# Normalised pixels in a ring of six parts, more buffers, a third accumulated tap in some jobs, and 6 of 11 bands of one convolution chunk on TensorE

## The chip, the core and the metric

The kernel runs on one core of a Trainium2 chip. The core has five engines that follow their own instruction queues in order: TensorE (PE in the profile; its weight loads are PEld), VectorE (DVE), ScalarE (ACT), GpSimd (POOL) and SyncE (SP). Waits on semaphores tie the queues together. The metric is the device time of one execution in microseconds (us).

## What is computed

The input is x, 16 images of 128 channels and 96 x 96 pixels in float32. Per image:

```python
xn1 = layernorm(x, ln1_w, ln1_b)                    # over the 128 channels of each pixel
q, k, v = xn1 @ wq.T, xn1 @ wk.T, xn1 @ wv.T        # 8 heads of 16 channels
attn = softmax(einsum('bhcn,bhdn->bhcd', l2norm(q), l2norm(k)) * 16**-0.5)   # over pixels n
x = x + (attn @ v) @ wp.T
xn2 = layernorm(x, ln2_w, ln2_b)
h1 = einsum('bchw,oc->bohw', xn2, w_in)             # 128 -> 512 hidden channels
h2 = depthwise_conv3x3(h1, w_dw)                    # 9 taps per channel, zero padding
x = x + einsum('bchw,oc->bohw', gelu(h2), w_out)    # 512 -> 128
```

The attention is between channels, so all of it is held in a Gram matrix of 128 x 128 per image, and its result is one 128 x 128 matrix per image that is multiplied with the normalised pixels.

## The kernel before

An image is cut into 8 bands of 12 rows, and a band into 3 units of 4 rows (384 pixels). The 512 hidden channels are 4 chunks of 128. One band and one chunk make a job. The program is laid down by a planner: each operation is registered with a place on a common scale, an estimated duration, the tokens that it reads and writes, and the buffers that it takes; a list scheduler then fixes the order of each engine's queue. The places are the table AT, in units of jobs. They are fixed in the source; nothing is scheduled while the kernel runs.

For each pixel block the first and second normalisation (suffix _a and _b) run: transpose (`forth`), statistics on VectorE, a power on GpSimd, scaling on ScalarE, transpose back (`back`), and a copy into the padded image (`place`). The first one also feeds the Gram matrix (`gram`). After the attention of an image, `mix` multiplies its first-normalised pixels with the attention's matrix and adds x. The second normalisation writes its pixels over the first ones.

```python
PE_CHUNK = 3
PE_BANDS = (0, 2, 4, 6)
PE_OF = 7
# ...
DMA_TAPS = (1, 2)
QT = 4
H_BANKS = 4
X1_BUFS, XB_BUFS, PR_BUFS, H3_BUFS, ZT_BUFS = 2, 5, 4, 9, 3
# ...
    xns = [pad.tile([P, HP * WP + 2], F32, tag=f"xn{k}", name=f"xn{k}") for k in range(min(B, 2))]
# ...
    def interior(i, u):
        return window(xns[i % 2], 1 + u * UR, UR, 1)
```

The padded images `xns` are thus two buffers of a whole image each, used in turn. The convolution of a job has nine taps. Tap 0 and the taps in DMA_TAPS are products of ScalarE; the products of DMA_TAPS are summed by accumulating transfers (SBUF to SBUF, issued by GpSimd), and the other six taps are multiply-and-add instructions of VectorE:

```python
        def product(t):
            if t == 0:
                to = h3_of(g, n)
            else:
                to = d["pr", t] = prp.tile([P, BR, W], F32, tag="pr", name=f"pr_{g}_{n}_{t}")
            nc.scalar.activation(to, shifted(t), AF.Copy, scale=dw[:, n, t : t + 1])

        def tap(t):
            h3 = h3_of(g, n)
            nc.vector.scalar_tensor_tensor(h3, shifted(t), dw[:, n, t : t + 1], h3, ALU.mult, ALU.add)

        def add_products(t):
            to = d["pr", DMA_TAPS[0]] if t != DMA_TAPS[0] else h3_of(g, n)
            nc.gpsimd.dma_start(out=to, in_=d["pr", t], accum_op=ALU.add)
# ...
        last = j == len(jobs) - 1
        dma_taps = () if last else DMA_TAPS
        left = [t for t in range(1, 9) if t not in dma_taps]
# ...
        act(t_act(BR * W, 1), at("product", j), lambda: product(0), h1, h3)
        for k, t in enumerate(dma_taps):
            jk = j + STEP["products"] * k
            act(t_act(BR * W, 1), at("products", jk), lambda t=t: product(t), h1, [("pr", (jn, t))])
        pr = [("pr", (jn, t)) for t in dma_taps]
        for k, t in enumerate(dma_taps[1:]):
            add(at("add_last", j), lambda t=t: add_products(t), [pr[1 + k]], [pr[0]])
        for k, t in enumerate(left):
            dve(t_dve(BR * W), at("tap", j + STEP["tap"] * k), lambda t=t: tap(t), h1, h3, True)
        if dma_taps:
            add(at("add_first", j), lambda: add_products(DMA_TAPS[0]), [pr[0]], h3)
```

The chunk 3 of some bands goes another way: the 1 x 1 product and the 3 x 3 convolution are one matmul per tap, nine accumulating in PSUM, with no work for VectorE.

```python
        for t in range(9):
            dy = t // 3
            zs = z_units(i, r0 + dy, r0 + dy + UR)
            pe(t_mm(UT), at("conv", p + STEP["conv_tap"] * t), lambda t=t: product(t), [*zs, ("w", "conv")], [pc])
        act(t_act(UT), at("conv_gelu", p), gelu, [pc], [("h3", (g, PE_CHUNK), s)])
# ...
    def by_pe(g):
        return g % PE_OF in PE_BANDS

    NG = B * NB
    jobs, first = [], []
    for g in range(NG):
        first.append(len(jobs))
        jobs += [(g, n) for n in range(NCH) if n != PE_CHUNK or not by_pe(g)]
```

Then `ffn_out` multiplies the four chunks of a unit with w_out, VectorE adds the result to x, and a band is stored.

Of the kernel before, what the change touches and what calls it, by code (L numbers as in the profile page):

```python
# [20 lines left out]
PE_BANDS = (0, 2, 4, 6)  # L21
PE_OF = 7
TINY = 1e-20
DMA_TAPS = (1, 2)
QT = 4
H_BANKS = 4
X1_BUFS, XB_BUFS, PR_BUFS, H3_BUFS, ZT_BUFS = 2, 5, 4, 9, 3
IN_TURN = ("tr", "h3", "pr", "xb", "x1")
AT = dict(
    weights=0.9, zeros=6.55, load_a=-14.05, forth_a=-8.8, stats_a=-11.5, variance_a=-13.4, power_a=3.35,  # L30
    shift_a=-4.85, scaled_a=-0.8, gram=-2.9, back_a=-19.8, place_a=-18.9, attention=-9.75, mix=-10.05,
    residual=-13.2, mixed=-4.5, add_x=4.65, forth_b=-6.15, stats_b=1.25, variance_b=-4, power_b=-19,
    shift_b=-16.6, scaled_b=0.85, back_b=-14.75, place_b=-1.75, halo=1.55, hidden=-0, kept=-5.25,
    product=-4.6, products=2.35, add_last=-9.55, tap=6, add_first=25.15, gelu=-2.6, conv=1.9,
    conv_gelu=-2.9, out=2.85, add=5.05, store=1.6,
)
STEP = dict(hidden=0.1, products=0.5, tap=0.166, conv=1.6, conv_tap=0.03, out=0.8, out_part=0.05)
# [3 lines left out]
WAIT = dict(POOL=350, SP=1300, ACT=1300)  # L41
T_ADD, T_MOVE = 3100, 1800


class Plan:
# [44 lines left out]
    def order(self):  # L90
# [38 lines left out]
        def dispatch(engine, time):  # L129
            queue = queues[engine]  # L130
            while queue:
                item = heapq.heappop(queue)
                k = item[1]
                lacks = room(k)
                if lacks is None:
                    break
                waiting.setdefault(lacks, []).append(k)
            else:
                return
            o = ops[k]  # L140
            starts[k] = time
            idle[engine] = False
            for t in o[5]:
                self.slot[t] = free[t[0]].pop(0)
                if t[0] in IN_TURN:
                    turn[t[0]].pop()
                    wake(t[0], time)
            ns, result, own = o[1], o[6], o[7]
            if o[8]:
                self.dma = max(time + ns + WAIT[engine], self.dma) + o[8]  # L150
                result = own = self.dma + result - time
            elif engine == "POOL":
                rest = self.two - time
                ns, result = (ns, result) if rest <= 0 else (rest + 705, rest + result)
                own = result
            if o[9]:
                self.two = time + ns + 35
            push(time + own, "own", k)
            push(time + ns, "idle", k)
            push(time + result, "done", k)  # L160
# [39 lines left out]
def tile_restormer_block(  # L200
# [33 lines left out]
    HP, WP = H + 2, W + 1  # L234
    D = C // HEADS
    assert PE_CHUNK == NCH - 1 and BR * W >= 8 * P and QT % 2 == 0 and NU * TPU % QT == 0 and C == P and UT % P == 0 and H % BR == 0 and NCH == 4
# [22 lines left out]
    mhalf = const.tile([P, QT], F32, name="mhalf")  # L259
# [25 lines left out]
    xns = [pad.tile([P, HP * WP + 2], F32, tag=f"xn{k}", name=f"xn{k}") for k in range(min(B, 2))]  # L285
# [20 lines left out]

    def interior(i, u):
        return window(xns[i % 2], 1 + u * UR, UR, 1)
# [21 lines left out]
    def z_units(i, r0, r1):  # L330

        lo, hi = min(max(r0 - 1, 0), H - 1) // UR, min(r1 - 2, H - 1) // UR
        return [("z", i % 2, u) for u in range(lo, hi + 1)]
# [29 lines left out]
    def zeros(p):  # L363


        def around(t, r):
            if r == HP:
                nc.gpsimd.memset(t[:, :WP], 0.0)
                nc.gpsimd.memset(t[:, (r - 1) * WP : r * WP], 0.0)
            nc.gpsimd.memset(t[:, : r * WP].rearrange("p (r w) -> p r w", w=WP)[:, :, :1], 0.0)  # L370
            nc.gpsimd.memset(t[:, r * WP :], 0.0)

        for t in zT_bufs:
            op("POOL", 300, at("zeros", p - 1), lambda t=t: nc.gpsimd.memset(t[:, :, P:], 1.0), [], [("w", "ones")], 500)
        for t, r in [(xns[0], HP)] + [(t, BR + 2) for t in h1s] + [(xn, HP) for xn in xns[1:]]:
            op("POOL", 1000, at("zeros", p), lambda t=t, r=r: around(t, r), [], [("w", "in")], 1200)

# [97 lines left out]
    def norm(i, second, place_of):  # L475
# [8 lines left out]
        def x2(s, u):  # L484
# [21 lines left out]
            ins = [("z", i % 2, u), ("m", i)]  # L506
# [10 lines left out]
        def pixels(s, q):  # L517

            d = {}
            tiles = range(q * QT, (q + 1) * QT)  # L520
            early = i == 0 and (not second or q < EARLY)
# [3 lines left out]
            def forth():  # L525
                if early:
                    d["pT"] = bank((name, q)).rearrange("p (t c) -> p t c", c=P)
                else:
                    d["pT"] = p_tr.tile([P, QT, P], F32, tag="tr", name=f"pT_{name}_{q}")
                for t in tiles:  # L530
                    b, j = divmod(t, TPB)
                    xt = (xbs if x_key(i, b, second) == "xb" else x1s)[i, b]
                    nc.tensor.transpose(d["pT"][:, t - tiles[0], :], xt[:, j * P : (j + 1) * P], ident)  # L533

            def stats(j):

                if j == 0:
                    d["st"] = small.tile([P, QT // 2, 6], F32, tag="st", name=f"st_{name}_{q}")
                nc.vector.bn_stats(  # L539
                    d["st"][:, j, :], d["pT"][:, 2 * j : 2 * j + 2, :].rearrange("p t c -> p c t")  # L540
                )

            def variance():
                d["mv"] = d["st"].rearrange("p j (t v) -> p (j t) v", v=3)
                ve = d["ve"] = small.tile([P, QT], F32, tag="ve", name=f"ve_{name}_{q}")
                nc.vector.tensor_scalar(ve, d["mv"][:, :, 2], 1.0 / C, EPS, ALU.mult, ALU.add)  # L546

            def power():
                rstd = d["rstd"] = small.tile([P, QT], F32, tag="rstd", name=f"rstd_{name}_{q}")
                nc.gpsimd.tensor_tensor(rstd, d["ve"], mhalf, ALU.pow)  # L550

            def shift():
                nb = d["nb"] = small.tile([P, QT], F32, tag="nb", name=f"nb_{name}_{q}")
                nc.vector.scalar_tensor_tensor(nb, d["mv"][:, :, 1], -1.0, d["rstd"], ALU.mult, ALU.mult)  # L554
                if by_dve:
                    take_zT()

            def take_zT():
                zTs[q] = zT_bufs[plan.slot["zT", (name, q)]]

            def also_scaled():
                for j in range(by_dve):
                    nc.vector.tensor_scalar(  # L563
                        zTs[q][:, j, :P], d["pT"][:, j, :], d["mv"][:, j, 1:2], d["rstd"][:, j : j + 1],
# [3 lines left out]
            def scaled():  # L568
                if not by_dve:
                    take_zT()  # L570
                zT = zTs[q]
                for j in range(by_dve, QT):
                    nc.scalar.activation(  # L573
                        zT[:, j, :P], d["pT"][:, j, :], AF.Identity,
                        bias=d["nb"][:, j : j + 1], scale=d["rstd"][:, j : j + 1],
                    )

            def gram():
                if q == 0:
                    grams[i] = p_g.tile([P, 4 * P], F32, tag="g", name=f"g_{i}")  # L580
                for t in tiles:
                    zt = zTs[q][:, t - tiles[0], :]
                    nc.tensor.matmul(  # L583
                        grams[i][:, : P + 1], lhsT=zt[:, :P], rhs=zt, start=(t == 0), stop=(t == NU * TPU - 1)
                    )

            tr, bt, zt = (key_, (name, q)), ("batch", (name, q)), ("zT", (name, q))
            units = {t // TPU: None for t in tiles}
            pe(110 * QT, at("forth" + ab, s), forth, [xtok(u) for u in units], [tr])
            for j in range(QT // 2):  # L590
                dve(341, at("stats" + ab, s), lambda j=j: stats(j), [tr], [bt])
            dve(80, at("variance" + ab, s), variance, [], [bt])
            op("POOL", 848, at("power" + ab, s), power, [], [bt], 881 + SLACK)
            dve(80, at("shift" + ab, s), shift, [], [bt, (*zt, 2)] if by_dve else [bt])
            if by_dve:
                dve(by_dve * 240, at("scaled" + ab, s), also_scaled, [tr, bt], [(*zt, 0)])
            act((QT - by_dve) * 343, at("scaled" + ab, s), scaled, [tr, bt], [(*zt, 1)])
            if not second:
                pe(QT * 220, at("gram", s), gram, [(*zt, 0), (*zt, 1), ("w", "ones")], [("g", i)])

        def channels(s, u):
# [14 lines left out]

            pb = ("bk", (name, u))
            quads = {(u * TPU + j) // QT: None for j in range(TPU)}
            pe(110 * TPU, at("back" + ab, s), back, [("zT", (name, q), k) for q in quads for k in range(2)], [pb])
            act(t_act(UT, 1) - 43 if second else t_copy(UT), at("place" + ab, s), place, [pb, ("w", "shift")], [("z", i % 2, u)])  # L620
# [7 lines left out]
        for q in range(NU * TPU // QT):  # L628
            pixels(place_of(q * QT), q)
            while u < NU and (u + 1) * TPU <= (q + 1) * QT:  # L630
# [3 lines left out]
    def attention(s, i):  # L634
# [4 lines left out]
        v = {}  # L639

# [4 lines left out]
        def ps(shape, tag):  # L645

            c = columns[tag]
            v[tag] = grams[i][: shape[0], c : c + shape[1]]
            return v[tag]

        def step(engine, ns, also=()):
            def add(f):
                op(engine, ns, s, f, [("w", "qk")], [("g", i), ("m", i), *also], ns + 200 + SLACK)
# [4 lines left out]
        @step("DVE", 210)  # L658
# [49 lines left out]
        @step("POOL", 848)  # L708
# [57 lines left out]
    def conv_job(j, g, n):  # L766

        i, b = divmod(g, NB)
        xn, r0 = xns[i % 2], b * BR
# [44 lines left out]
        dma_taps = () if last else DMA_TAPS  # L814
# [3 lines left out]
        for k, (r, e) in enumerate(chunks):  # L818
            ph = ("h", (jn, r))
            jk, zs = j + STEP["hidden"] * k, z_units(i, r0 + r, r0 + e)  # L820
# [20 lines left out]
    def by_matmuls(p, g, s):  # L841

        i, b = divmod(g, NB)
        xn = xns[i % 2]
        d = {}
        r0 = b * BR + s * UR
# [14 lines left out]
        for t in range(9):  # L861
            dy = t // 3
            zs = z_units(i, r0 + dy, r0 + dy + UR)
# [34 lines left out]
    def by_pe(g):  # L898
        return g % PE_OF in PE_BANDS
# [15 lines left out]
    for i in range(B):  # L915
# [4 lines left out]
        attention(at("attention", start2), i)  # L920
        norm(i, True, lambda t: start2 + band * t / TPB)
# [37 lines left out]
```

## Time and profile before

| | |
|---|---|
| device time, median of 3 executions | 4420.35 us (4417.46 to 4422.78) |
| span of the profiled execution | 4419.5 us |
| PE busy | 4309.8 us, 17782 matmuls |
| DVE busy | 4271.7 us, 5681 instructions |
| ACT busy | 4059.8 us, 7071 instructions |
| POOL busy | 1884.1 us, 1620 instructions |
| data moved by DMA | 744.52 MB, 168 GB/s on average |

A row of groups in the profile gives the source line, the engine, the operation, what it writes and reads, how often (x), its busy time in us and the mean duration of one in ns, and then the idle time of its engine just before it and who ended that. A row of waits gives who waited for whom: us in total, how often, the longest. A row of the timeline gives the start, the length, engine, line and operation, with equal neighbours merged (x6 is six instructions); in square brackets is the idle time before it. One instruction may begin before the one before it is shown as ended, so lengths of neighbours overlap. Line 803 is a tap on VectorE, 799 a product on ScalarE, 807 the accumulating transfers, 811 the GELU, 783 the hidden product and 788 its copy into the padded band, 853 the convolution on TensorE with its GELU in 859, 876 the product with w_out, and 883 the last add.

### The profile page before, as it was taken

The numbers are of one execution on the slowest core, as the hardware profiler recorded it, in microseconds if no ns is written. First come the engines' busy times: TensorE is split into PE (matmuls) and PEld (weight loads), VectorE is DVE, ScalarE is ACT, GpSimd is POOL, SyncE is SP. The second block draws the span as 40 slices with busy tenths as digits, with TensorE's granted clock in tenths as the row PEclk, the third lists the DMA queues.
The fourth block names the chain that finished last, engine by engine and source line by source line (L and its number), as shares of the span: only waits on it lengthen the run. The fifth ranks groups of instructions, "written<-read, shape, count | busy, mean of one in ns | idle before, by whom it ended". The sixth has DMA issues, their size and how long they took to land. (4 is left out here: it accounts for less than half of the span.)

```text
span 4419.5 us, 53360 instructions
## 1 busy us (share of the span) xinstructions
PE 4309.8 (98%) x17782; PEld 2750.3 (62%) x17782; DVE 4271.7 (97%) x5681; ACT 4059.8 (92%) x7071; POOL 1884.1 (43%) x1620
## 2 busy tenths in 40 slices
PE   7999999999999999999999999999999999999997
PEld 6656666666666666666666666666666666666554
DVE  6999999999999999999999999999999999999998
ACT  4999999999999999999999999999999999989885
POOL 3444444344444444444444444444435444444331
PEclk9999999999999999999999999999999999999998
DMA  2778888787888878788887887878888788878886
GB/s 78 160 162 177 172 175 179 166 181 158 182 172 172 183 166 176 168 171 180 167 176 167 179 173 163 181 167 179 173 171 177 167 181 168 171 171 162 171 166 134
DMA packets 183635, 744.52 MB, mean 168 GB/s; under 512 B 21312, under 2 KB 22720, under 8 KB 183360
## 3 DMA queue, kind: packets, MB, share of 16 engines
q0 software_dynamic: 143856, 589.30, 70.7%
q1 hardware_dynamic: 37152, 151.01, 9.4%
q8 instruction: 140, 2.29, 0.2%
q10 hardware_dynamic: 2352, 0.81, 0.1%
q14 instruction: 135, 1.11, 0.1%
HBM read 148.85 MB, written 75.50 MB: 51 GB/s over the span
## 5 line engine op out<-in xcount | busy, mean ns | idle before, releaser
L803 DVE SCALAR_TENSOR_TENSOR h<-h,dw,h 128x1152 f32<-128x1152 f32 x2636 | 3651.3, 1405 | 5.4 <-ACT h L799 1.0
L853 PE MATMUL h<-xn,comp 128*128 128x384 f32 x3942 | 1422.7, 486 | 8.2 <-ACT x L500 5.0
L799 ACT ACTIVATE pr<-h,dw 128x1152 f32<-128x1152 f32 x876 | 1131.1, 1301 | 31.3 <-DMA pr<-pr 30.7
L876 PE MATMUL h<-h,woutT 128*128 128x384 f32 x3072 | 1116.1, 492 | 41.3 <-ACT h L788 17.7
L783 PE MATMUL h<-xn,winT 128*128 128x384 f32 (+1 forms) x2634 | 1034.2, 500 | 5.7 <-ACT h L859 2.4
L853 PEld LDWEIGHTS h<-xn,comp 128*128 128x128 f32 x3942 | 719.4, 189 | 465.7 <-issue 17.1
L876 PEld LDWEIGHTS h<-h,woutT 128*128 128x128 f32 x3072 | 562.6, 192 | 400.9 <-ACT h L788 27.9
L807 POOL DMA_DIRECT2D h<-pr x438 | 408.1, 932 | 845.8 <-issue 154.3
L788 ACT COPY h<-h 128x384 f32<-128x384 f32 (+1 forms) x1317 | 655.0, 532 | 90.8 <-PE h L783 68.8
L807 POOL DMA_DIRECT2D pr<-pr x438 | 404.3, 923 | 752.0 <-ACT pr L799 611.8
L550 POOL TENSOR_TENSOR rstd_b<-ve_b,mhalf 128x4 f32<-128x4 f32 x288 | 524.1, 1820 | 380.4 <-DVE ve_b L546 354.1
L550 POOL TENSOR_TENSOR rstd_a<-ve_a,mhalf 128x4 f32<-128x4 f32 x288 | 509.2, 1773 | 388.4 <-DVE ve_a L546 376.1
L783 PEld LDWEIGHTS h<-xn,winT 128*128 128x128 f32 x2634 | 474.7, 190 | 304.6 <-issue 35.9
L811 ACT ACTIVATE h<-h 128x1152 f32<-128x1152 f32 x441 | 529.4, 1201 | 71.4 <-DMA h<-pr 68.6
L799 ACT ACTIVATE h<-h,dw 128x1152 f32<-128x1152 f32 x439 | 569.8, 1298 | 4.9 <-PE h L876 1.1
L573 ACT ACTIVATE zT<-pT_b,nb_b,rstd_b 128x128 f32<-128x128 f32 x1132 | 438.8, 510 | 14.6 <-DVE nb_b L554 13.6
L573 ACT ACTIVATE zT<-pT_a,nb_a,rstd_a 128x128 f32<-128x128 f32 x1080 | 417.5, 508 | 22.3 <-DVE nb_a L554 19.4
L583 PEld LDWEIGHTS g<-zT 128*128 128x128 f32 x2304 | 291.2, 191 | 40.2 <-issue 2.1
L583 PE MATMUL g<-zT 128*128 128x129 f32 x2304 | 304.8, 274 | 0.2 <-DVE zT L563 0.2
L491 PE MATMUL h<-xn,mwT 128*128 128x384 f32 x768 | 286.2, 489 | 3.2 <-ACT h L788 1.7
L613 ACT ACTIVATE xn<-pB_b,b 128x384 f32<-128x384 f32 x384 | 242.7, 632 | 24.4 <-PE pB_b L609 23.4
L539 DVE BATCH_NORM_STATS2 st_b<-pT_b 128x6 f32<-128x256 f32 x566 | 236.2, 420 | 6.2 <-PE pT_b L533 5.7
(111 smaller groups left out, 3237.3 us busy)
## 6 DMA issues: line engine op xcount, KB each, us to landing
pr<-pr POOLq DMA_DIRECT2D x438, 576.0 KB, 5.4
h<-pr POOLq DMA_DIRECT2D x438, 576.0 KB, 6.2
x<-in_x_dram SPq DMA_DIRECT2D x128, 576.0 KB, 5.5
out_dram<-x SPq DMA_DIRECT2D x127, 576.0 KB, 3.7
x<-in_x_dram POOLq DMA_DIRECT2D x123, 576.0 KB, 7.2
out_dram<-x SPq DMA_DIRECT2D x3, 192.0 KB, 1.8
weights<-in_L_conv_w_in_dram ACTq DMA_DIRECT2D x1, 256.0 KB, 10.6
weights<-in_L_conv_w_out_dram ACTq DMA_DIRECT2D x1, 256.0 KB, 10.7
```

Of the source, the lines that this page charges most:

```text
L491: nc.tensor.matmul(rows(pm), lhsT=mats[i][0], rhs=interior(i, u), start=True, stop=True)
L550: nc.gpsimd.tensor_tensor(rstd, d["ve"], mhalf, ALU.pow)
L573: nc.scalar.activation(zT[:, j, :P], d["pT"][:, j, :], AF.Identity, bias=d["nb"][:, j : j + 1], scale=d["rstd"][:, j : j + 1],)
L583: nc.tensor.matmul(grams[i][:, : P + 1], lhsT=zt[:, :P], rhs=zt, start=(t == 0), stop=(t == NU * TPU - 1))
L783: nc.tensor.matmul(rows(ph), lhsT=winT[:, n, :], rhs=window(xn, r0 + r, e - r, 1), start=True, stop=True)
L788: nc.scalar.copy(window(h1_, r, e - r, 1), rows(d.pop(("ph", r))))
L799: nc.scalar.activation(to, shifted(t), AF.Copy, scale=dw[:, n, t : t + 1])
L803: nc.vector.scalar_tensor_tensor(h3, shifted(t), dw[:, n, t : t + 1], h3, ALU.mult, ALU.add)
L807: nc.gpsimd.dma_start(out=to, in_=d["pr", t], accum_op=ALU.add)
L811: nc.scalar.activation(h3, h3, AF.Gelu)
L853: nc.tensor.matmul(d["pc"], lhsT=comp[:, t, :], rhs=window(xn, r0 + dy, UR, dx), start=(t == 0), stop=(t == 8),)
L876: nc.tensor.matmul(rows(d["po"]), lhsT=woutT[:, n, :], rhs=h3s[g, n][:, s * UR : (s + 1) * UR, :], start=(k == 0), stop=(k == NCH - 1),)
```

## The change

There are several parts.

1. `xns` becomes a ring of six buffers of 24 rows (with a padding row above and below), so that one image takes four of them. Rows next to a cut are needed in both neighbours, so the second normalisation copies the edge row a second time (`place_row`), and the outer rows of an image are set to zero again for every image (`ends`). The memory that this frees goes to the pools: one more buffer for x bands (5 to 6), for products (4 to 5) and for the taps' sums (9 to 10).
2. In chunk 1 of every other band, tap 3 is a third accumulated product in place of a tap on VectorE.
3. Chunk 3 goes to TensorE in 6 of 11 bands, counted from the end, where it was 4 of 7 counted from the start.
4. The attention of the first image works in a PSUM bank of its own and no longer in that of the Gram matrix.
5. All places of the planner's table, and some of its durations, are new.

The purpose is to shift work between VectorE, TensorE, ScalarE and the transfers.

```diff
-PE_BANDS = (0, 2, 4, 6)
-PE_OF = 7
+PE_BANDS = (0, 2, 4, 6, 8, 10)
+PE_OF = 11
 TINY = 1e-20
-DMA_TAPS = (1, 2)
-QT = 4
+DMA_TAPS = (1, 2, 3)
+THIRD, THIRD_OF, THIRD_CHUNK = (0,), 2, 1
+PART, Z_PARTS = 24, 6
+QT, QB = 4, 1
 H_BANKS = 4
-X1_BUFS, XB_BUFS, PR_BUFS, H3_BUFS, ZT_BUFS = 2, 5, 4, 9, 3
+X1_BUFS, XB_BUFS, PR_BUFS, H3_BUFS, ZT_BUFS = 2, 6, 5, 10, 3
 IN_TURN = ("tr", "h3", "pr", "xb", "x1")
 AT = dict(
-    weights=0.9, zeros=6.55, load_a=-14.05, forth_a=-8.8, stats_a=-11.5, variance_a=-13.4, power_a=3.35,
-    shift_a=-4.85, scaled_a=-0.8, gram=-2.9, back_a=-19.8, place_a=-18.9, attention=-9.75, mix=-10.05,
-    residual=-13.2, mixed=-4.5, add_x=4.65, forth_b=-6.15, stats_b=1.25, variance_b=-4, power_b=-19,
-    shift_b=-16.6, scaled_b=0.85, back_b=-14.75, place_b=-1.75, halo=1.55, hidden=-0, kept=-5.25,
-    product=-4.6, products=2.35, add_last=-9.55, tap=6, add_first=25.15, gelu=-2.6, conv=1.9,
-    conv_gelu=-2.9, out=2.85, add=5.05, store=1.6,
+    weights=13.95, zeros=3.15, load_a=-16.5, forth_a=-13.65, stats_a=-3.7, variance_a=-8.5, power_a=2.25,
+    shift_a=-7.7, scaled_a=-1.8, gram=-2.7, back_a=-20.15, place_a=-18.95, attention=-16.9, mix=-10.45,
+    residual=-13.95, mixed=-8.95, add_x=12.85, forth_b=-11.4, stats_b=-5.65, variance_b=-8.6,
+    power_b=-18.6, shift_b=-25.05, scaled_b=-1.65, back_b=-21.6, place_b=-2.25, halo=2.3, hidden=-0.85,
+    kept=-5.15, product=-7.7, products=3.3, add_last=-8.75, tap=4.45, add_first=25.8, gelu=-10.75,
+    conv=0.1, conv_gelu=-5.7, out=3.25, add=-0.45, store=1.1,
 )
-STEP = dict(hidden=0.1, products=0.5, tap=0.166, conv=1.6, conv_tap=0.03, out=0.8, out_part=0.05)
+STEP = dict(scaled=0.3, hidden=0.1, products=0.5, tap=0.166, conv=1.6, conv_tap=0.03, out=0.8, out_part=0.05)
 SLACK = 300
 NORM1_END = 6.0
 EARLY = 5
 WAIT = dict(POOL=350, SP=1300, ACT=1300)
+T_POWER = 1000
 T_ADD, T_MOVE = 3100, 1800
 
 
@@ buffers @@
     pad = ctx.enter_context(tc.tile_pool(name="pad", bufs=1))
-    xns = [pad.tile([P, HP * WP + 2], F32, tag=f"xn{k}", name=f"xn{k}") for k in range(min(B, 2))]
+    xns = [pad.tile([P, (PART + 2) * WP + 2], F32, name=f"xn{k}") for k in range(Z_PARTS)]
     small = ctx.enter_context(tc.tile_pool(name="small", bufs=4))
     att = ctx.enter_context(tc.tile_pool(name="att", bufs=1))
@@ @@
 
+    def part_of(i, r):
+
+        return (i * PARTS + r // PART) % Z_PARTS, r % PART
+
     def interior(i, u):
-        return window(xns[i % 2], 1 + u * UR, UR, 1)
+        k, r = part_of(i, u * UR)
+        return window(xns[k], r + 1, UR, 1)
+
+    def z_unit(i, u):
+        k, r = part_of(i, u * UR)
+        return ("z", k, r // UR)
 
     def rows(t):
         return t.rearrange("p (r w) -> p r w", w=W)
@@ zero rows of every image @@
             op("POOL", 1000, at("zeros", p), lambda t=t, r=r: around(t, r), [], [("w", "in")], 1200)
+
+    def ends(p, i):
+
+        for r, at_, u in ((0, 0, -1), (H - 1, PART + 1, UPP)):
+            k = part_of(i, r)[0]
+            row = window(xns[k], at_, 1, 1)
+            op("POOL", 400, at("zeros", p), lambda row=row: nc.gpsimd.memset(row, 0.0), [], [("z", k, u)], 600)
 
     def weights(p):
@@ second normalisation: edge rows twice @@
 
+            def place_row(k, r, row):
+                to = window(xns[k], r, 1, 1)
+                nc.scalar.activation(to, rows(d["pB"])[:, row : row + 1, :], AF.Identity, bias=b2)
+
+            copies = []
+            if second and u % UPP == 0 and u > 0:
+                copies.append((part_of(i, u * UR - 1)[0], PART + 1, 0, UPP))
+            if second and u % UPP == UPP - 1 and u < NU - 1:
+                copies.append((part_of(i, (u + 1) * UR)[0], 0, UR - 1, -1))
+
             pb = ("bk", (name, u))
             quads = {(u * TPU + j) // QT: None for j in range(TPU)}
             pe(110 * TPU, at("back" + ab, s), back, [("zT", (name, q), k) for q in quads for k in range(2)], [pb])
-            act(t_act(UT, 1) - 43 if second else t_copy(UT), at("place" + ab, s), place, [pb, ("w", "shift")], [("z", i % 2, u)])
+            act(t_act(UT, 1) - 43 if second else t_copy(UT), at("place" + ab, s), place, [pb, ("w", "shift")], [z_unit(i, u)])
+            for k, r, row, of in copies:
+                act(225, at("place" + ab, s), lambda k=k, r=r, row=row: place_row(k, r, row), [pb, ("w", "shift")], [("z", k, of)])
+
 
         for u in range(0, NU if not second else 0, UPB):
@@ attention of the first image @@
         v = {}
+        apart = i == 0
+        mine = [("h", ("attention", i)) if apart else ("g", i), ("m", i)]
 
         def sb(shape, tag, pool=att):
             c = columns[tag]
-            v[tag] = grams[i][: shape[0], c : c + shape[1]]
+            v[tag] = (bank(("attention", i)) if apart else grams[i])[: shape[0], c : c + shape[1]]
             return v[tag]
 
         def step(engine, ns, also=()):
@@ jobs @@
         last = j == len(jobs) - 1
-        dma_taps = () if last else DMA_TAPS
+        third = n == THIRD_CHUNK and g % THIRD_OF in THIRD
+        dma_taps = () if last else DMA_TAPS[: 3 if third else 2]
         left = [t for t in range(1, 9) if t not in dma_taps]
         h1 = [("h1", n, k) for k in range(4)]
         h3 = [("h3", jn, s) for s in range(UPB)]
         for k, (r, e) in enumerate(chunks):
@@ bands on TensorE @@
 
     def by_pe(g):
-        return g % PE_OF in PE_BANDS
+        return (NG - 1 - g) % PE_OF in PE_BANDS
 
     NG = B * NB
     jobs, first = [], []
```

The rest of the diff passes these names through the code and lets the pixel groups be batched (QB = 1 keeps their size).

## The prediction

> **What bounds the kernel now.** I read the page's first part, then the busy time by stage, because a share over the whole span mixes filling, steady work and draining. The second fence's columns are stage, length, busy time of PE, PEld, DVE, ACT and POOL with instruction counts, clock, DMA share and GB/s.
>
> ```profile
> PE 4309.8 (98%) x17782; PEld 2750.3 (62%) x17782; DVE 4271.7 (97%) x5681; ACT 4059.8 (92%) x7071; POOL 1884.1 (43%) x1620
> ```
>
> ```profile
> 0.00:100.00 100.00, 72.68 (x477) 59.35 (x478) 58.88 (x212) 42.08 (x102) 32.69 (x59) 0.93 0.27 86
> 100.00:200.00 100.00, 95.42 (x406) 61.05 (x405) 93.87 (x126) 93.98 (x169) 41.95 (x34) 0.98 0.67 138
> 200.00:4200.00 4000.00, 3955.14 (x16312) 2522.12 (x16311) 3916.39 (x5148) 3763.76 (x6560) 1753.63 (x1471) 1.00 0.83 172
> 4200.00:4420.00 220.00, 186.51 (x591) 107.74 (x589) 202.58 (x198) 159.97 (x243) 55.85 (x56) 0.92 0.72 149
> ```
>
> In the steady 4000 us TensorE idles 45 us, VectorE 84, ScalarE 236, and the DMA engines move data 83% of the time. So there are two bounds side by side, PE and DVE, and a third engine with only 6% left. No one stage is slow; the rate of the whole is what the change must move.
>
> Next, what one instruction costs on a full engine. The groups give durations; the timeline gives the distance between starts, which is what a removed instruction gives back.
>
> ```profile
> L803 DVE SCALAR_TENSOR_TENSOR h<-h,dw,h 128x1152 f32<-128x1152 f32 x2636 | 3651.3, 1405 | 5.4 <-ACT h L799 1.0
> L853 PE MATMUL h<-xn,comp 128*128 128x384 f32 x3942 | 1422.7, 486 | 8.2 <-ACT x L500 5.0
> L799 ACT ACTIVATE pr<-h,dw 128x1152 f32<-128x1152 f32 x876 | 1131.1, 1301 | 31.3 <-DMA pr<-pr 30.7
> ```
>
> ```profile
> 2000.66 2.10 PE L853 MATMUL h<-xn,comp 128*128 128x384 f32 x6
> 2002.60 0.49 PE L609 MATMUL pB_a<-ident,zT 128*128 128x128 f32 x3
> ...
> 2023.52 2.43 ACT L799 ACTIVATE pr<-h,dw 128x1152 f32<-128x1152 f32 x2
> 2025.82 0.50 ACT L615 COPY xn<-pB_a 128x384 f32<-128x384 f32 x1
> ...
> 4371.78 10.71 DVE L803 SCALAR_TENSOR_TENSOR h<-h,dw,h 128x1152 f32<-128x1152 f32 x8
> ```
>
> Six matmuls occupy PE for 1.94 us (2000.66 to the next start at 2002.60), 0.323 us each and not the 0.486 of the group. Two ScalarE products take 2.30 us, 1.15 each and not 1.30. Eight VectorE taps take 10.71 us including the last one's full 1.41, so (10.71 - 1.41) / 7 = 1.33 each.
>
> The third view is what ScalarE waits for, then the DMA queues:
>
> ```profile
> ACT h L788 <- PE h L783: 68.8, 127, 2.0
> ACT h L811 <- DMA h<-pr: 68.6, 63, 7.8
> ACT pr L799 <- DMA pr<-pr: 30.7, 30, 3.6
> ```
>
> ```profile
> q0 software_dynamic: 143856, 589.30, 70.7%
> q1 hardware_dynamic: 37152, 151.01, 9.4%
> ```
>
> The GELU waits 63 times for the accumulating transfer, and the product 30 times for a free product buffer. These are the places where more buffers could help and more transfers could hurt. Last, the end of the timeline:
>
> ```profile
> 4389.13 15.32 DVE L803 SCALAR_TENSOR_TENSOR h<-h,dw,h 128x1152 f32<-128x1152 f32 x11
> 4405.06 10.93 PE L876 MATMUL h<-h,woutT 128*128 128x384 f32 x24 [16.66 <-ACT h L811]
> 4416.02 0.56 DVE L883 TENSOR_TENSOR x<-h,x 128x384 f32<-128x384 f32 x1 [2.02 <-PE h L876]
> ```
>
> After the last tap at 4404.4 come 24 matmuls in a row at 0.455 us, an add and a store: 15 us in which only one engine works at a time.
>
> **What the Trainium skill says.** Perfetto Trace Analysis, section Identifying the Most-Contended Engine, warns that the busy share of matmuls is not a good measure of TensorE, while occupancy is fair for VectorE and ScalarE. This trace agrees: 0.486 us shown against 0.323 us of pace. Section Optimizing Scalar/DVE Operations of the same page says that the write-acknowledge half of a shown duration overlaps with the next instruction; here this is 0.15 us of a 1.30 us product. DMA: Bandwidth & Descriptors, section SWDGE vs HWDGE vs iDMA, says that accumulating transfers can be issued from GpSimd alone and share the 16 DMA engines with all other transfers; the trace has all of them in q0, at 70.7%, beside 9.4% in q1. SBUF — State Buffer, section Who interferes with whom, says that a VectorE instruction with two SBUF inputs and a GpSimd instruction that reads SBUF lock each other out. Here GpSimd pays: its power takes 1.01 us at the start, before any tap runs, and 1.8 us on average later, while the tap stays at 1.40. So added GpSimd work need not slow the taps.
>
> **The change part by part.** Counts are from the two programs' instruction lists. One product in the program is two matmuls in the trace.
>
> Bands on TensorE fall from 73 to 70 (of 128). That removes 3 x 27 = 81 products, 162 matmuls x 0.323 = 52.3 us, and adds three ordinary jobs: 3 hidden products of 384 and 6 of 480 columns, 6 x 0.323 + 12 x 0.40 = 6.8 us. PE: -45.5 us.
>
> The third accumulated tap is in 64 jobs. VectorE would have 3 x 6 = 18 more taps for the three jobs and loses 64: 2636 to 2590, -46 x 1.33 = -61 us. Three more residual adds of the first image (six bands of x are loaded at once instead of five), 3 x 0.53, give back 1.6. DVE: -59.6 us.
>
> ScalarE gets 64 + 6 = 70 more products, 70 x 1.15 = 80.5 us; three first products, 3.5; three GELUs at 1.07, 3.2; copies of the hidden rows, 3 x 0.37 + 6 x 0.46 = 3.9. It loses nine short GELUs (3.3) and three mixes (1.4). The parts need their neighbour's edge row twice: 96 row copies. A copy of 192 elements takes 0.25 us in the timeline and one of 384 takes 0.36, so 96 elements take about 0.2, and a bias adds 0.1 (placing with and without it: 0.47 and 0.37). 96 x 0.3 = 28 us, an estimate. ACT: +114 us.
>
> Accumulating transfers rise from 999 to 1068. q0's 70.7% of 4419.5 is 3125 us, 3.13 each; 69 more are 216 us. All queues together go from 3553 us (80.4%) to about 3770, 86% of a span of 4370. GpSimd gains 69 issues at 0.92, about 64 us plus 32 short memsets; at 45% it bounds nothing.
>
> The last band moves to TensorE. In the new order only three products of the output, six matmuls, stand behind the last GELU instead of twelve products. So of the 15 us after the last tap about 5 stay: -10 us, all on the end. The 27 products it needs fit into the 16.7 us that PE waited there. The first image's attention gets its own bank; in the order VectorE's softmax no longer stands behind statistics that waited for a load. Two us at the start, an estimate.
>
> Sum for the steady 4000 us (90.5% of the work): PE 3955 - 41 = 3914, DVE 3916 - 54 = 3862, ACT 3764 + 104 = 3868. If PE keeps its 45 us of idle time the stage lasts 3959. DVE then has 97 us of slack and ACT 91, so ScalarE must idle no more than VectorE does today. I expect that most of this works but not for nothing, and add 8 us of friction. Whole: 4420 - 45.5 - 10 - 2 + 8 = 4370.5; I say 4370.
>
> **Rivals.** First, ScalarE becomes the bound. If it kept all 236 us of its idle time the stage would take 3868 + 236 = 4104 and the kernel some 4520. Against it: its waits are short and spread, and none over 8 us in the steady part; an engine ahead of its suppliers shows such waits without needing them. If 150 us stay, the stage is 4018 and the kernel about 4425.
>
> Second, the transfers. At 86% the queue is longer, the GELU's 68.6 us and the product's 30.7 us of waiting grow, and a job with three transfers in a row holds its buffers for 5.4 + 5.4 + 6.2 = 17 us. For it: median landing times already exceed the 3.13 us of work. Against it: one buffer more in each of three pools. If these waits doubled, +100 us on ScalarE would mean 4400 to 4440.
>
> Third, the ring of six parts starves the first normalisation. Two whole images become one and a half, so pixels of the next image wait until convolution leaves a part. Against it: in ScalarE's program order, in two middle images, the first normalisation stands 27 to 35 units of four rows ahead of the convolution before, and 28 to 35 after. I give it 5%.
>
> Fourth, it goes better: more buffers and new places remove waits, and the time follows VectorE: 4420 - 60 - 10 - 2 = 4348, and less if VectorE's 84 us of idle time shrink too. A third less would be 4320.
>
> **Range and chances.** The middle is 4370; the fourth rival without friction marks the low end, 4345; half of the first or second marks the high end, 4405. Faster by over 2% means under 4332 and needs both PE and DVE to lose waits: 0.07. Slower by over 2% means above 4509, ScalarE keeping all its idle time: 0.02. Within 2%: 0.91.
>
> **What would show it.** Right: 3780 conv matmuls and 2590 taps at unchanged durations; ACT at 95 to 96% of the span; DMA share of the steady part near 0.88; six matmuls after the last GELU. PE's idle share in the steady part near 1.1 to 1.4%. Wrong: ScalarE's idle time in the steady part staying over 150 us with PE or DVE waiting for it; GELU waits for transfers well over 100 us; or placing of first-normalised pixels held up by the convolution.

## The result and the profile after

The changed kernel takes 4349.83 us (median, 4347.69 to 4352.01) against 4420.89 us in the same comparison: ratio 0.984, interval 0.9823 to 0.9857. Predicted were 4370 us in a range of 4345 to 4405.

The same views as before, now of the changed kernel. Busy time by engine, and by stage (length, then busy time of PE, PEld, DVE, ACT, POOL; clock; DMA share; GB/s):

```profile
PE 4261.9 (98%) x17638; PEld 2717.5 (62%) x17638; DVE 4212.9 (97%) x5638; ACT 4136.9 (95%) x7240; POOL 1964.4 (45%) x1725
```

```profile
0.00:100.00 100.00, 77.47 (x504) 64.47 (x505) 61.45 (x221) 45.48 (x112) 34.56 (x68) 0.90 0.27 86
100.00:200.00 100.00, 98.08 (x420) 62.72 (x419) 95.48 (x126) 98.46 (x179) 43.68 (x35) 1.00 0.73 147
200.00:4200.00 4000.00, 3957.81 (x16326) 2516.90 (x16326) 3913.37 (x5164) 3886.16 (x6798) 1852.02 (x1587) 1.00 0.89 185
4200.00:4351.00 151.00, 128.56 (x392) 73.45 (x390) 142.59 (x129) 106.85 (x155) 34.14 (x36) 0.94 0.76 158
```

In the steady 4000 us TensorE idles 42 us (45 before), VectorE 87 (84) and ScalarE 114 (236). The idle time that ScalarE had has been filled with work, and the other two did not lose by it. The groups, with tap, convolution and product in new line numbers:

```profile
L838 DVE SCALAR_TENSOR_TENSOR h<-h,dw,h 128x1152 f32<-128x1152 f32 x2590 | 3588.1, 1408 | 10.1 <-ACT h L834 6.9
L889 PE MATMUL h<-xn,comp 128*128 128x384 f32 x3780 | 1365.1, 486 | 2.2 <-ACT h L823 2.2
L834 ACT ACTIVATE pr<-h,dw 128x1152 f32<-128x1152 f32 x946 | 1290.5, 1389 | 3.9 <-DMA pr<-pr 3.6
```

ScalarE's waits and the queues:

```profile
ACT h L823 <- PE h L818: 49.2, 72, 3.3
ACT h L846 <- DMA h<-pr: 48.5, 42, 9.2
...
ACT pr L834 <- DMA pr<-pr: 3.6, 7, 0.7
```

```profile
q0 software_dynamic: 153792, 630.00, 76.7%
q1 hardware_dynamic: 37152, 151.01, 9.6%
```

More is transferred, and yet the wait for a product buffer fell from 30.7 to 3.6 us and the GELU's wait for the transfer from 68.6 to 48.5. Last, the end of the timeline:

```profile
4342.26 1.41 DVE L838 SCALAR_TENSOR_TENSOR h<-h,dw,h 128x1152 f32<-128x1152 f32 x1
4345.46 1.85 DVE L919 TENSOR_TENSOR x<-h,x 128x384 f32<-128x384 f32 x3 [1.79 <-PE h L912]
```

The last tap ends at 4343.7, 6.6 us before the end of the span at 4350.3; before it was 15.

### The profile page after: what moved, and what is told of

Its sections match the earlier page's. It is cut to its first block, busy times and chain, and to the rows that moved or that the text cites. A ratio compares the mean times of both kernels' runs of the same rounds, so it can differ in the third digit from the quotient of the medians.

```text
span 4350.3 us, 53308 instructions
## 1 busy us (share of the span) xinstructions
PE 4261.9 (98%) x17638; PEld 2717.5 (62%) x17638; DVE 4212.9 (97%) x5638; ACT 4136.9 (95%) x7240; POOL 1964.4 (45%) x1725
## 5 line engine op out<-in xcount | busy, mean ns | idle before, releaser
L838 DVE SCALAR_TENSOR_TENSOR h<-h,dw,h 128x1152 f32<-128x1152 f32 x2590 | 3588.1, 1408 | 10.1 <-ACT h L834 6.9
L889 PE MATMUL h<-xn,comp 128*128 128x384 f32 x3780 | 1365.1, 486 | 2.2 <-ACT h L823 2.2
L834 ACT ACTIVATE pr<-h,dw 128x1152 f32<-128x1152 f32 x946 | 1290.5, 1389 | 3.9 <-DMA pr<-pr 3.6
L912 PE MATMUL h<-h,woutT 128*128 128x384 f32 x3072 | 1149.2, 489 | 13.2 <-ACT h L823 4.8
L818 PE MATMUL h<-xn,winT 128*128 128x384 f32 (+1 forms) x2652 | 1051.6, 503 | 25.1 <-ACT h L823 14.2
L889 PEld LDWEIGHTS h<-xn,comp 128*128 128x128 f32 x3780 | 689.7, 189 | 431.4 <-issue 9.2
L842 POOL DMA_DIRECT2D pr<-pr x505 | 461.9, 915 | 823.0 <-ACT pr L834 656.5
L823 ACT COPY h<-h 128x384 f32<-128x384 f32 (+1 forms) x1326 | 727.6, 607 | 61.6 <-PE h L818 49.2
L818 PEld LDWEIGHTS h<-xn,winT 128*128 128x128 f32 x2652 | 472.3, 190 | 331.4 <-issue 47.9
L846 ACT ACTIVATE h<-h 128x1152 f32<-128x1152 f32 (+1 forms) x444 | 561.4, 1265 | 50.6 <-DMA h<-pr 48.5
L834 ACT ACTIVATE h<-h,dw 128x1152 f32<-128x1152 f32 x442 | 603.3, 1366 | 5.4 <-PE h L912 3.3
L634 ACT COPY xn<-pB_a 128x384 f32<-128x384 f32 x384 | 237.2, 618 | 23.9 <-PE pB_a L628 23.7
```

Of the source, the lines that this page charges most:

```text
L818: nc.tensor.matmul(rows(ph), lhsT=winT[:, n, :], rhs=window(xn, r0 + r, e - r, 1), start=True, stop=True)
L823: nc.scalar.copy(window(h1_, r, e - r, 1), rows(d.pop(("ph", r))))
L846: nc.scalar.activation(h3, h3, AF.Gelu)
L889: nc.tensor.matmul(d["pc"], lhsT=comp[:, t, :], rhs=window(xn, r0 + dy, UR, dx), start=(t == 0), stop=(t == 8),)
L912: nc.tensor.matmul(rows(d["po"]), lhsT=woutT[:, n, :], rhs=h3s[g, n][:, s * UR : (s + 1) * UR, :], start=(k == 0), stop=(k == NCH - 1),)
```

## The experiments

Two theories stand against each other. Work: the time follows what TensorE and VectorE have to do, and the rest only allows it. Order and buffers: the new places and the added buffers brought the gain. The comparisons below are with the kernel before on the same chip.

### First, one part undone or done alone, nothing else touched

The work alone on the kernel before:

```diff
-PE_BANDS = (0, 2, 4, 6)
-PE_OF = 7
+PE_BANDS = (0, 2, 4, 6, 8, 10)
+PE_OF = 11
-DMA_TAPS = (1, 2)
+DMA_TAPS = (1, 2, 3)
+THIRD, THIRD_OF, THIRD_CHUNK = (0,), 2, 1
# and third, dma_taps and by_pe as in the change
```

> The kernel before with two parts alone: the third accumulated tap (64 jobs) and the bands on TensorE (6 of 11 from the end). Ring, buffers and places stay old. If the time follows the work on TensorE and VectorE: 4420 - 45 (TensorE) - 8 (end) = about 4367, at most 4380. If the gain came from order and buffers: within 10 us of 4420, or above because the old places do not fit the new work.

Measured: 4481.42 us, ratio 1.0137 (1.0122 to 1.0152). Slower by 60 us, on the side that the second expectation left open ("or above").

The changed kernel without the third tap:

```diff
-THIRD, THIRD_OF, THIRD_CHUNK = (0,), 2, 1
+THIRD, THIRD_OF, THIRD_CHUNK = (), 2, 1
```

> The changed kernel without the third accumulated tap: VectorE gets 64 taps x 1.33 = 85 us back (4213 to 4298 busy), ScalarE loses 64 products (74 us), the transfers lose 200 us. If the work decides: VectorE bounds it and the time is 4350 + 85 less some of its 137 us of idle time, 4390 to 4435. If order and buffers decide: 4350 to 4370, since less work is on ScalarE and the transfers.

Measured: 4417.84 us, ratio 0.9993 (0.9984 to 1.0001). This fits the work theory, but as the next two show it need not be the work alone: the places had been made for other instructions.

The changed kernel with the old table of places:

```diff
 AT = dict(
-    weights=13.95, zeros=3.15, load_a=-16.5, forth_a=-13.65, ...
+    weights=0.9, zeros=6.55, load_a=-14.05, forth_a=-8.8, ...     # all entries as before the change
```

> The changed kernel with the old table of places. Same instructions in another order. If the work decides: 4355 to 4375. If the new order brought the gain: 4400 or more.

Measured: 4507.15 us, ratio 1.0197 (1.0182 to 1.0213). The same instructions in another order cost 157 us.

The changed kernel with the old numbers of buffers:

```diff
-X1_BUFS, XB_BUFS, PR_BUFS, H3_BUFS, ZT_BUFS = 2, 6, 5, 10, 3
+X1_BUFS, XB_BUFS, PR_BUFS, H3_BUFS, ZT_BUFS = 2, 5, 4, 9, 3
```

> The changed kernel with the old numbers of buffers (5 x bands, 4 products, 9 sums). If the work decides: 4350 to 4360. If the buffers absorb the transfers that came on top (ScalarE waits for product buffers and for the transfer before the GELU): 4380 or more, and these waits back at 30 us and 70 us or above.

Measured: 4596.56 us, ratio 1.0395 (1.038 to 1.0411), 247 us over the changed kernel. ScalarE's two waits are at 40.4 us (product buffers) and 78.0 us (the GELU), as expected if the buffers absorb the transfers. Who else waits in it, on PE and then on DVE (who for whom: us in total, times, longest):

```profile
PE h L818 <- ACT h L823: 52.4, 32, 4.5
PE h L912 <- ACT h L846: 37.0, 23, 10.1
```

```profile
DVE x L919 <- PE h L912: 70.1, 55, 4.7
DVE h L838 <- ACT h L834: 60.7, 41, 6.5
```

These waits stand at 14.2, 4.4, 11.8 and 6.9 us in the changed kernel. The queues are fixed in the source, so a place that suits ten buffers makes an engine stand in front of an instruction that with nine is not ready. Such an experiment measures the part that was undone and the misfit of the order together, and the misfit is larger than everything to be explained: of the 247 us here, 213 went away when the same kernel got places of its own (4383 us, below). The first four runs do not separate the theories.

### Second, the same with the places searched anew

So each variant got places of its own: entries of AT were changed at random, and kept when the kernel's planner put the last instruction earlier. The planner chose the order only; all times are the chip's. Four kernels make a square: old or new work, old or new memory. "New memory" is the ring and the added buffers, and with them all else that the change brought: the edge copies, the bank of the first attention and the planner's new durations.

Old work, old memory: the kernel before with only AT changed.

> The kernel before with nothing changed but its places, searched anew with the kernel's own planner for this set of instructions. Control for how much new places alone can bring. If places alone brought the gain of the change: 4370 or less. If the work and the buffers matter: 4405 to 4425.

Measured: 4409.45 us, ratio 0.9978 (0.997 to 0.9986).

Old work, new memory: the changed kernel with

```diff
-PE_BANDS = (0, 2, 4, 6, 8, 10)
-PE_OF = 11
+PE_BANDS = (0, 2, 4, 6)
+PE_OF = 7
-THIRD, THIRD_OF, THIRD_CHUNK = (0,), 2, 1
+THIRD, THIRD_OF, THIRD_CHUNK = (), 2, 1
-        return (NG - 1 - g) % PE_OF in PE_BANDS
+        return g % PE_OF in PE_BANDS
 AT = dict(   # searched anew
```

> Ring of parts, more buffers and edge copies of the change, but the taps and bands of the kernel before; places searched anew for it. If ring and buffers bring the gain by themselves: 4360 to 4380. If the work on TensorE and VectorE decides: 4395 to 4420, because that work is the old one.

Measured: 4384.85 us, ratio 0.9927 (0.9912 to 0.9942), between the two expectations.

New work, old memory: the first experiment's edit with AT searched anew.

> The kernel before with the third accumulated tap and the new bands, old ring and old buffers, places searched anew for it (with the old places it took 4481). If only the fit of the places was missing there: 4365 to 4380, near the changed kernel. If the extra transfers need the extra buffers: 4385 to 4420, with ScalarE and GpSimd waiting for product buffers and transfers.

Measured: 4389.18 us, ratio 0.9935 (0.9919 to 0.9952). The fit of the places was worth 92 us here (4481 to 4389), but the kernel is not near the changed one. ScalarE's waits in it:

```profile
ACT pr L800 <- DMA pr<-pr: 44.0, 47, 3.0
ACT pr L800 <- DMA h<-pr: 40.8, 38, 2.7
```

85 us of waiting for a product buffer to be read out by a transfer, where the changed kernel has 3.6. The expectation had this sign right. Its steady stage has TensorE idle 68 us and VectorE 113:

```profile
200.00:4200.00 4000.00, 3932.41 (x16200) 2493.89 (x16198) 3886.50 (x5126) 3832.16 (x6655) 1804.28 (x1543) 1.00 0.88 183
```

New work, new memory: the changed kernel with only AT changed.

> The changed kernel with its places searched further. Tells how far its own places were from the best: 4330 to 4348 if search still brings some tenths of a per cent; 4350 or above if the places are at their best on the chip.

Measured: 4337.87 us, ratio 0.9818 (0.9804 to 0.9833). 12 us under the changed kernel: its own places were near the best, not at it. The steady stages of the other three corners, in the order old work with old memory, old work with new memory, new work with new memory:

```profile
200.00:4200.00 4000.00, 3963.06 (x16363) 2533.99 (x16362) 3923.62 (x5158) 3777.19 (x6572) 1728.89 (x1474) 1.00 0.83 173
200.00:4200.00 4000.00, 3968.81 (x16412) 2537.57 (x16411) 3929.33 (x5181) 3797.22 (x6699) 1778.69 (x1510) 1.00 0.83 173
200.00:4200.00 4000.00, 3964.58 (x16363) 2520.13 (x16362) 3924.72 (x5173) 3893.07 (x6822) 1858.07 (x1589) 1.00 0.89 185
```

| places searched anew | old memory | new memory |
|---|---|---|
| old work | 4409 us | 4385 us |
| new work | 4389 us | 4338 us |

The work brings 20 us without the buffers and 47 with them; the memory 25 us without the work and 51 with it; the places alone 9 (4418.7 of the kernel before in that comparison, to 4409.5). The sum of the two single effects is 45, both together 72. The rest, 27 us, is there only when both are. This fits the view that the extra transfers need the buffers, and that the buffers are used best by the extra transfers. A search ends at a different distance from the best order in each corner, so a part of each number is the search's. How large it is was not measured. The tables hint at unequal starts: the searched kernels with old buffers keep conv = 1.9 of the old table, the others are at or near the 0.1 of the new one, which had been fitted to the new work and the new memory already. So a part of the 27 us may be the better start. Nor were the two halves of the work, the third tap and the bands, tried apart with fitted places.

### Third, which part of the memory, and what is next

Ring kept, buffers old (5, 4, 9), places searched anew:

> The changed kernel, with ring and the new work, but the old numbers of buffers (5, 4, 9), places searched anew for it. If the buffers make room for the extra transfers: 4380 to 4400, as the kernel before with the new work and fitted places (4389), with ScalarE waiting some 80 us for product buffers again. If the ring itself or something else in the change makes the difference: 4340 to 4355.

Measured: 4383.19 us, ratio 0.9915 (0.99 to 0.993). So the ring by itself does little for the time (4383 with it, 4389 without, both with old buffers; how much of the 6 us is the search's is not known); it pays by the memory that it frees. ScalarE's waits for transfers, here and then in the changed kernel with places searched anew:

```profile
ACT pr L837 <- DMA pr<-pr: 25.4, 29, 3.5
ACT h L849 <- DMA h<-pr: 16.8, 25, 1.5
ACT pr L837 <- DMA h<-pr: 15.5, 15, 3.6
```

```profile
ACT h L846 <- DMA h<-pr: 57.1, 44, 8.1
ACT pr L834 <- DMA pr<-pr: 12.1, 12, 2.7
```

The waits for product buffers are 41 us, half of what was expected. Together with the GELU's the slower kernel waits less for transfers (58 us) than the faster one (69). So the sum of these waits does not tell what the buffers are worth. TensorE's idle time in the steady stage does: 56 us here, 35 there, and of this the waits that ScalarE ended are 49 and 29 us.

```profile
200.00:4200.00 4000.00, 3944.48 (x16256) 2505.93 (x16256) 3893.05 (x5133) 3865.74 (x6761) 1869.21 (x1576) 1.00 0.88 183
```

A likely reading is that a wait before a product holds up what ScalarE has to do next for TensorE, and a wait before a GELU does so less. No run tests this.

Only the product buffers old:

```diff
-X1_BUFS, XB_BUFS, PR_BUFS, H3_BUFS, ZT_BUFS = 2, 6, 5, 10, 3
+X1_BUFS, XB_BUFS, PR_BUFS, H3_BUFS, ZT_BUFS = 2, 6, 4, 10, 3
 AT = dict(   # searched anew
```

> The changed kernel with 4 product buffers instead of 5, the other two pools as in the change, places searched anew. If the product buffers alone matter: 4375 to 4390. If the three pools share the effect: 4345 to 4362.

Measured: 4351.98 us, ratio 0.9843 (0.9827 to 0.986): 14 us of the 45 between 4338 and 4383, as expected if the three pools share the effect. Its ScalarE waits for product buffers again:

```profile
ACT pr L834 <- DMA h<-pr: 28.3, 30, 5.5
ACT pr L834 <- DMA pr<-pr: 27.7, 28, 3.1
```

These 56 us are 12 in the re-searched kernel, but the GELU's wait fell to 12.9, so the sum is 69 us in both. TensorE's idle time in the steady stage is 43 us instead of 35. The other two pools were not undone one by one.

Edge rows copied four times instead of once, places searched anew:

```diff
-            for k, r, row, of in copies:
+            for k, r, row, of in 4 * copies:
```

> The changed kernel with each copy of an edge row made four times (288 more short copies on ScalarE, which write the same values), places searched anew. 288 x 0.27 = 78 us more work on ScalarE alone. If ScalarE has become a bound: 4390 or more. If TensorE and VectorE bound the time: 4338 to 4352, with ScalarE's idle time about 70 us shorter.

Measured: 4352.62 us, ratio 0.9847 (0.9832 to 0.9862). The rows of the copies and of the engines:

```profile
L638 ACT ACTIVATE xn<-pB_b,b 128x96 f32<-128x96 f32 x384 | 203.0, 529 | 0.3
```

```profile
PE 4268.9 (98%) x17638; PEld 2716.5 (62%) x17638; DVE 4210.7 (97%) x5638; ACT 4193.8 (96%) x7528; POOL 1958.5 (45%) x1725
```

ScalarE is busy 63.5 us more than in the re-searched kernel (4130.3), 0.22 us for each of the 288 copies (mostly 0.22 to 0.24 us is also the distance from such a copy's start to the next start in the timeline between 2035 and 2130 us, where the mean shown duration is 0.529). The time grew by 15 us (4337.9 to 4352.6), just past the upper edge of what was expected if ScalarE is no bound. TensorE's idle time in the steady stage stayed at 36 us (35 before), ScalarE's fell from 107 to 57. So ScalarE's work is no longer free, but about a quarter of it, some us of which may be the search's, reaches the time; it is not the bound.

One step further in the same direction:

```diff
-PE_BANDS = (0, 2, 4, 6, 8, 10)
-PE_OF = 11
+PE_BANDS = (0, 2, 4, 6, 8, 10, 12)
+PE_OF = 13
-THIRD, THIRD_OF, THIRD_CHUNK = (0,), 2, 1
+THIRD, THIRD_OF, THIRD_CHUNK = (0, 2), 3, 1
```

Its places:

```python
AT = dict(
    weights=28.8, zeros=73.95, load_a=-13.05, forth_a=-13.45, stats_a=-36.1, variance_a=8.85, power_a=-3.8,
    shift_a=-21.4, scaled_a=-1.1, gram=-2.95, back_a=-48, place_a=-95.7, attention=-18.6, mix=-12.1,
    residual=1.35, mixed=-29, add_x=26.1, forth_b=-11.4, stats_b=-3.1, variance_b=-0.7, power_b=-35.45,
    shift_b=-26.1, scaled_b=-0.35, back_b=-21.4, place_b=-2.15, halo=1.15, hidden=-0.85, kept=-13.6,
    product=-5.95, products=3.65, add_last=-76.5, tap=78, add_first=42.05, gelu=7, conv=0.1, conv_gelu=-4.8,
    out=3.1, add=9.8, store=11.1,
)
```

> One step further in the same direction: 7 of 13 bands on TensorE (69 instead of 70) and the third accumulated tap in two of three bands (85 jobs, last one excepted), places searched anew. TensorE loses 27 x 2 x 0.323 - 2.3 = 15 us, VectorE 21 - 6 = 15 taps, 20 us; ScalarE gets 21 + 2 products and a job, about 33 us, the transfers 23 x 3.1 = 71 us. If TensorE and VectorE still bound: 4320 to 4332. If transfers or ScalarE bound by now: 4338 or more.

Measured: 4322.91 us, ratio 0.9778 (0.9764 to 0.9793), as expected if TensorE and VectorE bound. This is the fastest of all, 27 us under the changed kernel and 15 under its re-searched form. TensorE is still the engine that idles least:

```profile
PE 4240.2 (98%) x17590; PEld 2708.0 (63%) x17590; DVE 4187.3 (97%) x5623; ACT 4158.2 (96%) x7265; POOL 2035.8 (47%) x1748
```

```profile
200.00:4200.00 4000.00, 3964.02 (x16359) 2524.48 (x16359) 3912.31 (x5175) 3930.17 (x6864) 1929.90 (x1615) 1.00 0.91 189
```

In its steady stage ScalarE idles 70 us, less than VectorE (88), and the transfers are at 91%. By these numbers there is little left to shift.

## Why the prediction held, and where it was off

TensorE's ledger can be held against the sum of the prediction term by term, since its busy time and idle time make up the span. Idle time by part: the first 200 us, the steady stage (4000 us before, 3930 after), and the last 220 us.

| term | predicted | measured |
|---|---|---|
| TensorE's work | -45.5 | -47.9 (4309.8 to 4261.9) |
| the end | -10 | -7.4 (33.0 to 25.6 idle) |
| the start | -2 | -7.5 (31.9 to 24.5 idle) |
| friction in the steady stage | +8 | -6.5 (44.9 to 38.4 idle) |
| sum | -49.5 | -69.3 |

The first row is not the work alone. The same 17638 matmuls show 4257 to 4340 us of busy time in the runs with the new work, the 17782 of the old work 4298 to 4310, depending on the order. With places searched anew the difference is 31 us with the old memory and 41 with the new, so the -47.9 next to -45.5 looks closer than it is.

**The counts were right.** 3780 convolution matmuls and 2590 taps; VectorE's busy time fell by 58.8 us (59.6 predicted), TensorE's by 47.9. Taking the distance between starts rather than the shown duration made this possible: 162 matmuls at the shown 0.486 would have been 79 us.

**The end was right in kind and size.** From the last tap to the end it is 8.4 us less. That only six matmuls follow the very last GELU could not be read off: the timeline merges twelve of them after 4342.58, with the last band's GELUs beside them. One step of the sum was slightly off: the 27 products of the last band are 54 matmuls of 0.323 us, 17.4 us, and do not quite fit into the 16.7 us that TensorE waited.

**ScalarE's busy time rose by less than predicted,** by 77 us in place of 114. One part is the edge copy, 0.22 us in place of 0.3, 8 us in all. The rest is how busy time is counted. The last instruction before a gap counts with its whole shown duration, which is longer than its distance to a next start, and ScalarE has 411 gaps now where it had 730. An estimate from the two traces: counted by the median distance between starts of its form, ScalarE's work grew by 107 us (3941 to 4048), and the ends that run out into gaps shrank by 37 (100 to 63). So the work was predicted well, and the busy time shows less of it.

**The step that failed is the friction.** I let ScalarE and the transfers cost TensorE and VectorE 8 us as they fill up, and gave the added buffers no term of their own. They filled up as predicted (ScalarE 95% of the span, transfers 0.89 of the steady stage), and the idle time of TensorE fell all the same, to 1.05% of the steady stage, just under the 1.1 to 1.4 that I had named. The square shows two effects against each other. TensorE's idle time in the steady stage, in us:

| places searched anew | old memory | new memory |
|---|---|---|
| old work | 36.9 | 31.2 |
| new work | 67.6 | 35.4 |

With the old memory the friction is there and larger than I said, 31 us; with the new memory it is 4. The fall below the 45 us of the kernel before is not the buffers' doing alone: new places by themselves bring that kernel to 37. What I had as the fourth rival, 4348, is where it went, and waits that buffers and places remove are what the square shows. VectorE's sum fits that rival as well (58.8 us less work, 10 less idle time), but TensorE still idles less than VectorE, so that the time follows VectorE is not shown. The start was under-sized too. The changed kernel with old places, which has the separate bank as well, has a TensorE busy time of 170.9 us in the first 200, against 175.6 in the changed one and 168.1 before; so more of the start seems to come from the places than from the bank. With places searched anew it is 166.6 and 169.0 with the old memory, 173.1 and 175.0 with the new, and 168.7 with the ring and the bank but old buffers, so the added buffers may have a part. The bank by itself was not undone.

**The rivals.** ScalarE as the bound is out: 63.5 us more of it cost 15. The transfers: the queue is longer (a transfer of products lands after 6.4 us in the median, 5.7 before), and the waits whose doubling I feared fell from 99 to 52 us. With the new work and the old memory they are 104 us, with the ring and old buffers 58, so the rival was sound as to the need for buffers and not as to the size of the waits. The ring does not starve the first normalisation: with it, the new work and old buffers the kernel takes 4383 us, without it 4389, and in the changed kernel ScalarE waits 23.7 us before placing first-normalised pixels, all of it for TensorE's transposes (34.4 before).

**What was missing in the reasoning** is the order. I took the new places as part of the scenery. The runs show that the wrong places cost 157 us, twice the whole effect, and that a shift of work without new places is a loss of 60 us. The prediction came out right because the change brought its own fitting places; it had no reason to count on that, and here it was lucky.

## What to carry over

In a kernel whose engines' queues are fixed in advance and nearly full, a part can't be valued by undoing it alone: each variant needs its own order, and then the parts show what they are worth, and that they need each other. A shift of work to an engine with slack pays the distance between starts of the instructions removed on the full engines, provided the buffers between the engines grow with the traffic: here 45 us were counted on TensorE, and the shift was worth 20 without the new memory and 47 with it. When the engine that takes the work comes near 95%, measure the price of more work on it directly, as with the repeated copies: here it was about 15 us for 63.5.

## What the runs showed of the hardware that was not expected

ScalarE's shown durations grow while it runs without a gap, though its pace does not. In the changed kernel, rows of its timeline:

```profile
1999.61 1.16 ACT L846 ACTIVATE h<-h 128x1152 f32<-128x1152 f32 x1 [0.95 <-DMA h<-pr]
...
2001.30 1.25 ACT L834 ACTIVATE pr<-h,dw 128x1152 f32<-128x1152 f32 x1
2002.45 0.57 ACT L632 ACTIVATE xn<-pB_b,b 128x384 f32<-128x384 f32 x1
...
2018.39 1.40 ACT L834 ACTIVATE pr<-h,dw 128x1152 f32<-128x1152 f32 x1
2019.54 0.63 ACT L895 ACTIVATE h<-h 128x384 f32<-128x384 f32 x1
...
2027.66 1.49 ACT L834 ACTIVATE h<-h,dw 128x1152 f32<-128x1152 f32 x1
2028.82 1.73 ACT L588 ACTIVATE zT<-pT_b,nb_b,rstd_b 128x128 f32<-128x128 f32 x4
```

Soon after a gap a product is shown with 1.25 us, 17 us later with 1.40, 26 us later with 1.49 (tap 0, which writes the sum itself), and each time the next instruction starts 1.15 or 1.16 us after it. Over all 946 products of this group the mean is 1.26 us when the last gap is less than 5 us back and 1.53 when it is 30 to 60 us back, at a median distance to the next start of 1.16 in both; in the kernel before it is 1.26 and 1.48, at 1.15. So the mean of the group rose from 1.301 to 1.389 us with the change although the instruction became no slower: a longer mean on a fuller ScalarE is no sign of contention.
